# The first load of each slot in runs of 16 KB, the second in runs of 32 KB

## The chip, the cores and the metric

The kernel runs on one core of one Trainium2 chip. The metric is the device time of one execution in microseconds (us). An execution that the hardware profiler records gives a span, from the first instruction to the last, and a trace of every instruction and every DMA packet.

Five engines matter here. TensorE (PE) multiplies; VectorE (DVE) copies the products out of PSUM; ScalarE (ACT) issues the loads and moves data within SBUF; SyncE (SP) issues the stores; GpSimd (POOL) passes on that a buffer is free. Sixteen DMA engines carry the data between HBM and SBUF. ACT and SP each have a DMA queue of their own, and both queues are served by the same sixteen engines.

## The reference

For each of 128 batches one of eight weight matrices is chosen by `itok_B_0_7`, and its product is added to the input:

```python
B, C, D, T, N_SUBJECTS = (128, 128, 128, 1024, 8)
w = weights[subjects]
out = jnp.einsum('bct,bcd->bdt', x, w)
x = x + out
```

x and the output have 128 x 128 x 1024 float32 each, 67.11 MB in and 67.11 MB out. The weights are 0.52 MB.

## The kernel before

The work goes in 32 steps (`NT`) of four batches (`H * G`, two halves of two batches). One step's data is a slot: 2.10 MB of x, 16 KB in each of 128 partitions. SBUF holds 12 slots (`SLOTS`), used in turn. The product is written over the input in the same slot, and the residual is added by adding the identity matrix `eye` to the weights (line 195).

**Loads.** `load` (lines 147 to 154) issues two DMAs for a slot from ACT, one for each half h, 1 MB each. Two batches of x are one contiguous MB of HBM. `ROWS` says how the source is cut: eight rows of 4 KB make one run of 32 KB. The destination is 128 partitions with 8 KB each, so that partition p of a half has two neighbouring rows of a batch, whatever `ROWS` is. Both loads of a slot count on the same semaphore `s_in[k]`, and `landed` (line 160) waits for both.

**ACT's loop** (lines 273 to 291), for each slot in order: wait until the slot's loads have landed; wait on `s_empty` until the slot that is wanted next is free; issue the loads for the slot four steps ahead (`AHEAD`); then `trade` (lines 162 to 170), three copies within SBUF that bring the rows of one batch into one half. Four slots are loaded before the loop, and all of this is in ACT's program order: a slot that isn't free holds back the loads and also the trade behind them.

**PE** (lines 336 to 338) waits for the trade and the weights of a half and multiplies: eight matmuls a half, sixteen a slot. **DVE** (lines 330 to 335) copies the product of a half from PSUM into the slot (line 221) and prepares the next weights.

**Stores.** SP (lines 313 to 321) waits until a slot is finished and issues its store: 16 KB of SBUF per partition for one slot. The first store is written with another form (line 317), in rows of 4 KB. The last 12 slots are stored in pairs, and of these the last six slots in runs of 32 KB per partition (`WHOLE`). The very last store is issued on line 343.

**Free slots.** GpSimd waits for the store of each slot (line 311) and increments `s_empty`. So step i's loads, from step 12 on, wait for the store of step i - 12.

Of the kernel before, what the change touches and what calls it, by code (L numbers as in the profile page):

```python
# [30 lines left out]
G = 2  # L31
# [14 lines left out]

IDLE = 8

ROWS = 8

R = 2

# [12 lines left out]
def transfer(nc, engine, out, in_):  # L65

    later, nc._always_lower_symbolic_ap = nc._always_lower_symbolic_ap, False
    ins, outs = engine.lower_ap_dma(in_), engine.lower_ap_dma(out)  # L70
    nc._always_lower_symbolic_ap = later
    return engine.add_instruction(
        mybir.InstDMACopy(
            name=nc.get_next_instruction_name(),
            engine=engine.engine,
            ins=ins,
            outs=outs,
            mode="Copy",
            cce_op=ALU.bypass,
            queue=QUEUES[engine.engine],  # L80
        )
    )
# [3 lines left out]
def kernel(  # L86
# [60 lines left out]
    def load(k, slot, first):  # L147
        for h in range(H):
            transfer(
                nc,  # L150
                nc.scalar,
                x_all[:, bass.ds(slot * (H * G * T) + h * G * T, G * T)],
                x[bass.ds(first + h * G, G)].rearrange("h (b r) t -> (h b) (r t)", r=ROWS),
            ).then_inc(s_in[k], DMA)

    def move(out, in_):
# [66 lines left out]
    with tc.tile_critical():  # L223
# [44 lines left out]
        for i in range(AHEAD):  # L268
            load(i % AHEAD, i, i * (H * G))
# [3 lines left out]
        with nc.scalar.Fori(0, NT // AHEAD) as turn:  # L273
            for k in range(AHEAD):
                landed(k)
                with nc.scalar.If(turn < NT // AHEAD - 1):
                    empty = nc.scalar.wait_ge(s_empty, k + 1)
                    if k + 1 == AHEAD:
                        empty.then_inc(s_empty, -AHEAD)
                    load(  # L280
                        k,
                        (turn * AHEAD + (k + AHEAD)) % SLOTS,
                        nc.s_assert_within(
                            turn * (AHEAD * H * G) + (k + AHEAD) * H * G,
                            0,
                            B - H * G,
                            skip_runtime_bounds_check_because="the last turn loads nothing",
                        ),
                    )
                trade(k, (turn * AHEAD + k) % SLOTS)  # L290
            nc.scalar.wait_ge(s_moved, AHEAD * MOVES).then_inc(s_moved, -AHEAD * MOVES)
# [86 lines left out]
```

## Time and profile before

| What | us |
|---|---|
| three runs | 322.62, 322.94, 323.04 |
| their median | 322.94 |
| the profiled execution, its time | 323.06 |
| its span | 321.2 |
| PE matmuls busy | 250.1 (78%) |
| DVE busy | 181.4 (56%) |
| ACT busy | 183.6 (57%) |
| loads of x, median from issue to landing | 11.6 |

The span is what the trace covers; the profiled execution's own time is 1.9 us longer than it. The busy shares are means over the whole span and say nothing of which engine is waited for. The windows of the profile give the same for each stretch of time, with the busy share of the DMA engines and the rate at which they moved data as the last two columns. A packet's bytes are counted in the window in which it falls, so a rate in a short window can be off by some per cent either way.

The queue rows give, for one queue, its packets, its MB and the time that its packets took as a share of what sixteen engines have. q10 is ACT's queue, with the loads of x. q1 is SP's, with the stores, the weights and the list of subjects. Each DMA adds up to sixteen packets of 4 bytes, one from each engine, that report its completion.

### The profile page before, as it was taken

The numbers are of one execution on the slowest core, as the hardware profiler recorded it, in microseconds if no ns is written. First come the engines' busy times: TensorE is split into PE (matmuls) and PEld (weight loads), VectorE is DVE, ScalarE is ACT, GpSimd is POOL, SyncE is SP. The second block draws the span as 40 slices with busy tenths as digits, with TensorE's granted clock in tenths as the row PEclk, the third lists the DMA queues.
The fourth block names the chain that finished last, engine by engine and source line by source line (L and its number), as shares of the span: only waits on it lengthen the run. The fifth ranks groups of instructions, "written<-read, shape, count | busy, mean of one in ns | idle before, by whom it ended". The sixth has DMA issues, their size and how long they took to land. (4 is left out here: it accounts for less than half of the span.)

```text
span 321.2 us, 2576 instructions
## 1 busy us (share of the span) xinstructions
PE 250.1 (78%) x528; PEld 103.4 (32%) x528; DVE 181.4 (56%) x217; ACT 183.6 (57%) x98; POOL 2.5 (1%) x10
## 2 busy tenths in 40 slices
PE   7479998898899885949987499673997939999400
PEld 3134433333333332413433143231433414444100
DVE  4708766666677662660865627456273753877600
ACT  1577767776777726566454774547746379990000
POOL 0200000000000000000000000000000000000000
PEclk9969999999999997995999979998697998999955
DMA  8999999999999999999999999999999999999995
GB/s 314 404 457 424 420 403 436 408 433 445 426 424 426 435 414 430 437 430 441 433 402 426 416 433 441 428 418 422 426 439 441 408 453 408 426 445 418 433 428 228
DMA packets 7732, 134.76 MB, mean 420 GB/s; under 512 B 1457, under 2 KB 1458, under 8 KB 2098
## 3 DMA queue, kind: packets, MB, share of 16 engines
q1 hardware_dynamic: 4658, 67.64, 49.9%
q10 hardware_dynamic: 3072, 67.11, 49.0%
q14 instruction: 2, 0.02, 0.0%
HBM read 67.63 MB, written 67.11 MB: 419 GB/s over the span
## 5 line engine op out<-in xcount | busy, mean ns | idle before, releaser
L206 PE MATMUL ps<-x_all,w 128*128 x512 | 239.9, 627 | 48.7 <-PEq L202 48.7
L221 DVE COPY x_all<-ps 128x2048 f32 x64 | 146.6, 2291 | 116.1 <-PE ps L206 103.5
L206 PEld LDWEIGHTS ps<-x_all,w 128*128 128x128 f32 x512 | 99.3, 200 | 189.3 <-issue 189.2
L157 ACT COPY aside<-x_all 64x2048 f32 x32 | 60.7, 1897 | 95.0 <-issue 90.6
L157 ACT COPY x_all<-x_all x32 | 60.7, 1897 | 4.0
L157 ACT COPY x_all<-aside 64x2048 f32 x32 | 60.7, 1898 | 1.0
L195 DVE TENSOR_TENSOR w<-w_all,eye 128x128 f32<-128x128 f32 x132 | 31.8, 282 | 0.8 <-issue 0.8
L233 PE MATMUL ps<-x_all 128*128 128x512 f32 x16 | 10.2, 808 | 1.7 <-DVE x_all L230 1.7
L233 PEld LDWEIGHTS ps<-x_all 128*128 128x128 f32 x16 | 4.1, 262 | 6.9 <-issue 5.3
L271 ACT ACT_TABLE_LOAD x1 | 1.3, 1283 | 6.1 <-issue 6.1
L297 DVE COPY w_all<-x_all 32x256 f32<-32x256 f32 x12 | 3.9, 326 | 0.4
L242 DVE STREAM_TRANSPOSE x_all<-x_all 128x512 f32<-128x512 f32 x2 | 2.0, 1068 | 3.2 <-DMA x_all<-in_L_cond_weights_dram 3.2
L297 POOL COPY w_all<-x_all 32x256 f32<-32x256 f32 x4 | 1.7, 424 | 6.7 <-DVE x_all L294 6.6
L294 DVE STREAM_TRANSPOSE x_all<-x_all 128x1024 f32<-128x1024 f32 x1 | 1.2, 1226 | 0.0
L230 DVE MEMSET x_all<- 128x512 f32 x1 | 0.5, 485 | 1.0 <-SPq L223 1.0
L248 DVE TENSOR_SCALAR x_all<-x_all 1x128 int32<-1x128 int32 x1 | 0.2, 217 | 0.3 <-DMA x_all<-in_itok_B_dram 0.3
L258 POOL TENSOR_SCALAR_AFFINE_SELECT eye<-x_all 128x128 f32<-128x128 f32 x1 | 0.3, 292 | 1.4 <-DVE x_all L230 1.4
L252 DVE CUSTOM_DVE_ANT_0 index<-x_all 1x256 uint16<-1x256 uint16 x1 | 0.3, 280 | 0.0
L258 POOL TENSOR_SCALAR_AFFINE_SELECT eye<-eye 128x128 f32<-128x128 f32 x1 | 0.3, 292 | 0.1
L250 DVE TENSOR_SCALAR x_all<-x_all 1x128 int32<-1x128 int32 x1 | 0.2, 215 | 0.0
L271 ACT COPY mark<-eye 1x1 f32<-1x1 f32 x1 | 0.2, 190 | 0.0
L365 POOL MEMSET const-bfloat16-1.0<- 128x1 bf16 x1 | 0.1, 100 | 0.0
(5 smaller groups left out, 0.4 us busy)
## 6 DMA issues: line engine op xcount, KB each, us to landing
x_all<-in_x_dram ACTq DMA_DIRECT2D x64, 1024.0 KB, 11.6
out_dram<-x_all SPq DMA_DIRECT2D x20, 2048.0 KB, 55.0
out_dram<-x_all SPq DMA_DIRECT2D x6, 4096.0 KB, 30.9
x_all<-in_L_cond_weights_dram SPq DMA_DIRECT2D x1, 512.0 KB, 3.9
x_all<-in_itok_B_dram SPq DMA_DIRECT2D x1, 0.5 KB
```

Source lines behind the costliest of these rows:

```text
L157: nc.scalar.copy(out, in_).then_inc(s_moved, 1)
L195: copy = nc.vector.tensor_tensor(ws[q], w_all[:, bass.ds(subject[q], 1), :], eye, ALU.add)
L206: mm = nc.tensor.matmul(ps[h][:, q % G, t : t + N], ws[q][:, 0, :], x_all[:, bass.ds(at, N)], start=True, stop=True,)
L221: nc.vector.tensor_copy(mine, ps[h].rearrange("d g t -> d (g t)")).then_inc(s_added, 1)
L230: nc.vector.memset(zeros, 0.0).then_inc(s_zeros, 1)
L233: nc.tensor.matmul(ps[P_SLOTS - 1][:, G - 1, :N], zeros[:, :D], zeros, start=True, stop=True)
L242: nc.vector.transpose(w_mid.rearrange("p (e r h w j) -> p r j h e w", e=4, r=R, h=4, w=8)[:, r], w_raw.rearrange("p (j r d) -> p r j d", r ...
L252: nc.vector.tensor_tensor(index[:, :B], near, wrap, ALU.add).then_inc(s_index, 1)
L258: nc.gpsimd.affine_select(eye[:, 0], eye[:, 0] if r else zeros[:, :D], [[-1, D]], ALU.not_equal, 1.0, base=r - r * R * A, channel_multipli ...
L271: nc.scalar.copy(mark, eye[:1, 0, :1])
L294: nc.vector.transpose(w_late, w_mid).then_inc(s_sort, 1)
L297: engine.tensor_copy(w_all[32 * v : 32 * (v + 1), 2 * o : 2 * (o + 1), :], w_late[32 * o : 32 * (o + 1)].rearrange("c (e u r d) -> c u r e ...
```

## The change

`ROWS` becomes a list with a value for each half. The first load of a slot (h = 0) is cut into 64 runs of 16 KB, the second (h = 1) remains at 32 runs of 32 KB. Nothing else differs: the bytes, their places in SBUF, the order of the issues, the semaphores and their counts are the same.

```diff
-ROWS = 8
+ROWS = [4, 8]
...
                 x_all[:, bass.ds(slot * (H * G * T) + h * G * T, G * T)],
-                x[bass.ds(first + h * G, G)].rearrange("h (b r) t -> (h b) (r t)", r=ROWS),
+                x[bass.ds(first + h * G, G)].rearrange("h (b r) t -> (h b) (r t)", r=ROWS[h]),
             ).then_inc(s_in[k], DMA)
```

## The prediction

> **What bounds the kernel now.** I read the page first, its second and third parts, because they say which resource has no gaps.
>
> ```profile
> span 321.2 us, 2576 instructions
> ...
> DMA  8999999999999999999999999999999999999995
> ...
> DMA packets 7732, 134.76 MB, mean 420 GB/s; under 512 B 1457, under 2 KB 1458, under 8 KB 2098
> ...
> q1 hardware_dynamic: 4658, 67.64, 49.9%
> q10 hardware_dynamic: 3072, 67.11, 49.0%
> ...
> out_dram<-x_all SPq DMA_DIRECT2D x20, 2048.0 KB, 55.0
> ```
>
> The two queues together keep the 16 DMA engines busy for 98.9% of the span. q10 carries the loads of x: 67.11 MB, that is 64 loads of 1 MB. Its 3072 packets are 64 x 48, and 48 is 32 runs of 32 KB plus 16 completion writes (the packets under 512 B). So a packet of a load is one run of the source. q1 carries the stores and the weights; a store of 2 MB lands 55.0 us after its issue, five stores' worth of waiting. Next I read the windows, to see whether the DMA engines have slack in any stage:
>
> ```profile
> core 0: us, PE busy (x) PEld busy (x) DVE busy (x) ACT busy (x) POOL busy (x), PEclk, DMA share, GB/s
> 36.00:60.00 24.00, 21.57 (x50) 8.87 (x49) 16.72 (x21) 17.26 (x10) 0.00 (x0) 1.00 1.00 418
> 60.00:110.00 50.00, 45.94 (x105) 19.20 (x104) 34.30 (x37) 36.72 (x21) 0.00 (x0) 1.00 1.01 430
> 110.00:160.00 50.00, 38.69 (x79) 15.82 (x78) 25.81 (x31) 26.96 (x15) 0.00 (x0) 0.90 1.01 430
> 210.00:260.00 50.00, 40.32 (x82) 16.23 (x80) 27.83 (x32) 26.83 (x16) 0.00 (x0) 0.90 1.00 427
> 304.00:317.00 13.00, 0.00 (x0) 0.00 (x0) 0.00 (x0) 0.00 (x0) 0.00 (x0) 0.53 1.00 429
> 317.00:321.20 4.20, 0.00 (x0) 0.00 (x0) 0.00 (x0) 0.00 (x0) 0.00 (x0) 0.50 0.13 55
> ```
>
> The last two columns are what counts: share 1.00 or 1.01 and 418 to 430 GB/s in every stage up to 317 us, whether loads and stores are mixed or stores run alone. The compute engines have holes: PE 38.69 of 50 us in the third row, ACT 26.96. The bytes set the time: 134.76 MB at 428 GB/s are 315 us, and the rest of the span is the start and the completion of the last store.
>
> One other chain could become the bound, the one that ends in the issue of the last store. I followed it back by the timeline, the uses of line 311, and the waits of SP:
>
> ```profile
> L311 POOLq EVENT_SEMAPHORE  x1: 17/17/17, 256.1 to 256.1; - x1
> ...
> 256.47 1.16 ACTq L72 DMA_DIRECT2D x_all<-in_x_dram  x2
> 257.89 1.90 ACT L157 COPY aside<-x_all 64x2048 f32 x1 [6.32 <-issue]
> 264.12 36.39 PE L206 MATMUL ps<-x_all,w 128*128 x80 [5.04 <-PEq L202]
> 300.76 2.29 DVE L221 COPY x_all<-ps 128x2048 f32 x1 [0.79 <-DVEq L218]
> ...
> L72 SPq DMA_DIRECT2D out_dram<-x_all x25: 561/4571/12279, 36.2 to 303.7; - x25
> ...
> SPq L374 <- DMA out_dram<-x_all: 15.9, 1, 15.9
> ```
>
> At 256.1 us the store of slot 19 has landed; GpSimd passes this on (line 311), ACT issues the last two loads, then trades slot 27; PE works through five slots without a break; the last copy ends at 303.05 and SP issues the last store at 303.7. How much work the DMA engines still have then is told by the queue row of the stretch from 304 us to the end:
>
> ```profile
> q1 hardware_dynamic: 209, 5.80, 79.1%
> ```
>
> Of the 5.80 MB the last store is 4.19; 1.61 MB of the store before it had not begun, which at 427 GB/s cover 3.8 us. So the last store finds the engines busy, and this chain has slack.
>
> **The change, part by part.** Only line 153 differs. It moves no instruction, adds no wait, and leaves the bytes and their place in SBUF as they are (a slice of two batches is contiguous in HBM, however it is cut). For the 32 loads with h = 0 there are 64 runs of 16 KB in place of 32 runs of 32 KB: 32 x 32 = 1024 more packets, 64 on each of 16 engines. q10 should show 4096 packets.
>
> *The packets' price.* The trace has no load in 16 KB packets, so I bound it by the stores, which come in both sizes. These are the queue rows of three stretches with one kind of packet each: 272 to 288 us (stores in 16 KB), 292 to 312 us (stores in 32 KB), 10 to 29 us (loads in 32 KB):
>
> ```profile
> q1 hardware_dynamic: 432, 6.82, 100.2%
> ...
> q1 hardware_dynamic: 292, 8.52, 99.9%
> ...
> q10 hardware_dynamic: 383, 8.36, 102.3%
> ```
>
> 6.82 MB are 416 packets of 16 KB: 1.002 x 16 engines x 16 us / 416 = 616.6 ns each. 8.52 MB are 260 of 32 KB: 0.999 x 16 x 20 / 260 = 1229.5 ns each. Two small ones cost 2 x 616.6 - 1229.5 = 3.7 ns more than a large one. 1024 x 3.7 ns / 16 = 0.24 us. A load in 32 KB is quicker still: 1.023 x 16 x 19 / 255 = 1219.6 ns. The upper end takes the whole difference of the two queue totals as one of packet size: q1 cost 0.499 x 321.2 / 67.64 = 2.370 us per MB, q10 0.490 x 321.2 / 67.11 = 2.345; 0.0244 us x 33.55 MB (half of the loads) = 0.82 us. That includes the 4 KB packets of the weights and of the first store, so it is too high. The lower end is nothing: queues could hide the boundary. I take 0.24 us, since the same queue with the same kind of work gives it. None of it is hidden, because the engines have no gap.
>
> *The share of the two queues.* These are the rows of two stretches with both queues full: 100 to 104 us (loads in 32 KB beside stores in 16 KB) and 30 to 46 us (loads beside the first store, which goes in 4 KB rows):
>
> ```profile
> q10 hardware_dynamic: 52, 1.18, 68.8%
> q1 hardware_dynamic: 49, 0.54, 31.9%
> ...
> q10 hardware_dynamic: 271, 5.73, 84.9%
> q1 hardware_dynamic: 246, 1.01, 15.5%
> ```
>
> In the first, loads get 69% of the bytes, about 2 to 1: packet against packet. In the second, 85 to 15, near the 8 to 1 of 32 KB against 4 KB. So a shorter run takes a smaller turn. For a slot one engine's part of 128 KB will go in six turns (four of 16, two of 32 KB) in place of four, and six store packets (96 KB) pass beside it: loads get 128/224 = 57% in place of 67%, some 245 GB/s of 430 in place of 287. A slot of 2.10 MB takes 8.6 us in place of 7.3 while stores wait.
>
> The Trainium skill, page "DMA: Bandwidth & Descriptors", section "Queues, rings and completion order", also says that an engine goes round-robin between queue rows packet by packet, but its packet is typically 9 to 17 descriptors, not one run. Read so, both kinds of load would take turns of equal descriptor counts, 8 KB destination pieces against the stores' 4 KB ones, 2 to 1 before and after; the change would move no share. The trace speaks against it: 85 to 15 beside the first store, where that reading gives 67 to 33.
>
> Who waits for slower loads? These are ACT's issue of two slots' loads, and the issue row of the loads from 60 to 100 us (count, size, time to landing):
>
> ```profile
> 73.33 1.15 ACTq L72 DMA_DIRECT2D x_all<-in_x_dram  x2
> 81.01 1.15 ACTq L72 DMA_DIRECT2D x_all<-in_x_dram  x2
> ...
> x_all<-in_x_dram ACTq DMA_DIRECT2D x10, 1024.0 KB, 11.9
> ...
> ACT aside L157 <- issue: 64.2, 15, 6.3
> ```
>
> ACT asks for a slot each 7.7 us here, 273 GB/s, more than the 245 that loads will get, so they fall behind by 0.9 us a slot, 6 us over the 50 us to 110. A load is issued four slots, 31 us, before `landed` wants it, and lands 11.9 us after its issue: 19 us of cover. After 110 us (the last row is 110 to 260 us, 15 waits, 64.2 us of ACT) ACT waits for slots to be emptied; a period is there two slots' worth of bytes, 4.19 MB at 428 GB/s = 9.8 us, and a load of 8.6 us fits into it. What loads lose, stores win: they land earlier, and the engines stay full. Only without cover would ACT wait in `landed`, and even then the stores queued would keep the engines busy. At the end, store 19 lands when 20 stores and at most the 31 slots' loads issued by then have moved, as now; so the last store is issued no later than now but for the packet price. I cost the share at nothing.
>
> *Issue.* ACT's 64 issues could lengthen with more runs. SP issues its 32 KB stores, which have more pieces still, in 561 ns at least, against ACT's 501 to 512 ns: at most 0.06 us x 32 = 2 us on ACT, at least nothing. ACT's 64.2 us of waiting hide it. If the queue of loads filled up and held ACT back, as SP's issues are held (median 4571 ns), the same 19 us would cover it.
>
> **Sum.** 0.24 us on the DMA engines, nothing else. The profiled execution took 323.06 us (span 321.2, and 1.9 around it); it becomes 323.3. It lies 0.12 above the median of the three runs, 322.94, so the median becomes 323.2.
>
> **Rivals.**
> - *Dear packets (slower).* Place: every load with h = 0. Price: 0.82 us as above, 12.8 ns for each of 64 more packets on an engine; it decides from 10 ns, which makes 0.65 us. For it: no gap hides anything. Against it: 3.7 ns by the direct rows. Time 323.8.
> - *The last store comes late (slower).* If store 19 landed later than 256.1 by more than the 3.8 us of backlog less a start-up (the stores' first packets are not shown; I take 1 to 2 us), the engines would run dry before the last store. Each us beyond costs one: 1 to 2 us, 324 to 325. Against it: stores get more share, not less.
> - *The first store stops disturbing (faster).* From 36 to 60 us the engines move 418 GB/s, against 430 after: 24 x 12/430 = 0.67 us lost while the first store's 4 KB packets lie between 32 KB ones. With six turns for four it is through sooner. If all of this loss goes and packets cost nothing, 322.3; half of it with the packet price makes 322.8, no change. Against it: the small packets themselves stay.
> - *Nothing moves.* The queue cuts long runs by itself (3072 packets again), or it turns after equal counts of pieces, 8 KB of a load against 4 KB of a store, whatever the run: 322.9. Against it: packets of 32 KB as the run is now, and the 85 to 15. The second form is the Trainium skill's sentence read as above.
>
> **How the numbers follow.** A measurement of this kernel can tell about 0.2%, 0.65 us, from no change. The forecast (0.24 us, share moved, time unmoved) has 0.59; nothing moves 0.09; dear packets 0.12; a late last store 0.06; the first store 0.14. Same is 0.59 + 0.09 = 0.68, slower 0.12 + 0.06 = 0.18, faster 0.14. The range goes from the whole gain at the first store with 0.1 us for the runs' own spread, 322.2, to the dear packets with 0.3 us of a late last store, 324.1; beyond it lies most of the late store and a part of the first.
>
> **What would show it.** 4096 packets on q10 with the same MB; q10's share of the span up by about 0.1 of a point (0.24 of 321), not by 0.3; loads near 57 to 43 where both queues are full; loads landing later than 11.9 us and stores sooner than 55; DMA share still 1.00 from 60 to 317 us; SP's last issue at or before 304. Wrong would be: a DMA share under 0.98 after 300 us (late store), q10's time per MB up by over 1% (dear packets), or over 425 GB/s from 36 to 60 us with an earlier end.

## The result and the profile after

The changed kernel took 322.21 us (median of 14 runs, 321.81 to 322.96), the kernel before 322.93 us (14 runs, 322.30 to 323.17). The ratio is 0.9981, with a 95% interval of 0.9972 to 0.9989: faster by 0.19%, 0.6 us. In a second series of nine runs it was 0.9975 (0.9962 to 0.9988). The forecast was 0.24 us more. The profiled execution took 321.81 us, against 323.06.

The page of the changed kernel, its span, packets, queues and DMA issues (the last two rows end in the median time from issue to landing):

```profile
span 320.0 us, 2576 instructions
...
DMA packets 8757, 134.76 MB, mean 421 GB/s; under 512 B 1458, under 2 KB 1459, under 8 KB 2099
...
q1 hardware_dynamic: 4658, 67.64, 49.9%
q10 hardware_dynamic: 4096, 67.11, 49.3%
...
x_all<-in_x_dram ACTq DMA_DIRECT2D x64, 1024.0 KB, 15.8
out_dram<-x_all SPq DMA_DIRECT2D x20, 2048.0 KB, 55.1
```

q10 has the 4096 packets that were expected, so the change does what it says. Its packets took 0.493 x 320.0 = 157.8 us of all engines, against 0.490 x 321.2 = 157.4 before: a little more, as forecast, though the rounding of a share is worth 0.16 us in each. Loads land 4 us later. Yet the span is 1.2 us shorter. The next view is the queue rows (packets, MB, share of the 16 engines) from 60 to 100 us, first of the kernel before:

```profile
q10 hardware_dynamic: 475, 10.36, 60.4%
q1 hardware_dynamic: 472, 6.95, 40.8%
```

and of the changed one:

```profile
q10 hardware_dynamic: 552, 8.98, 52.5%
q1 hardware_dynamic: 555, 8.04, 47.3%
```

The loads' share fell from 60% to 53% of the engines' time. In both kernels the two queues have as many packets as each other, turn for turn, completions included; the loads' packets are smaller now.

Where did the time come from? The queue rows from 100 to 250 us show it. Of the kernel before:

```profile
q10 hardware_dynamic: 1485, 32.41, 50.6%
q1 hardware_dynamic: 2171, 31.64, 49.8%
```

and of the changed one:

```profile
q10 hardware_dynamic: 2071, 33.93, 52.9%
q1 hardware_dynamic: 2080, 30.41, 47.7%
```

The share times 16 engines times 150 us, divided by the MB, is what one MB costs an engine. Before: 0.506 x 2400 / 32.41 = 37.47 us for loads and 0.498 x 2400 / 31.64 = 37.78 for stores, 37.62 for both together. After: 37.42, 37.65 and 37.53. The rounding of a share is worth up to 0.04. So in these 150 us a MB became cheaper on both queues, although the loads have more packets and the stores the same ones. 0.09 us x 64.3 MB / 16 engines is 0.4 us of time.

The shares add up to slightly over 100%, so packets overlap a little, and packet time isn't quite time. The bytes say the same without it. With the bytes of each packet spread evenly over its time in the trace, the kernel before moved 64.14 MB in these 150 us and the changed one 64.32. At 428 GB/s, 0.18 MB are 0.4 us.

The engines were always busy before, but some packets took too long. The queue rows of three pairs of stretches of the kernel before show which ones; of each second stretch the loads' row alone. They are 177 to 181 and 181 to 183 us, then 137.5 to 141.3 and 141.3 to 143.3, then 255.7 to 260.4 and 260.4 to 262.4:

```profile
q1 hardware_dynamic: 115, 1.65, 99.0%
...
q10 hardware_dynamic: 19, 0.62, 80.8%
...
q1 hardware_dynamic: 101, 1.62, 100.4%
q10 hardware_dynamic: 2, 0.00, 0.0%
...
q10 hardware_dynamic: 21, 0.69, 83.9%
...
q1 hardware_dynamic: 124, 2.03, 101.6%
q10 hardware_dynamic: 11, 0.00, 0.1%
...
q10 hardware_dynamic: 19, 0.62, 72.4%
```

From 177 to 181 us there is no load at all: the loads' queue has run dry, and stores have the engines to themselves. When loads start again at 181 us, 19 of them take 0.808 x 16 x 2 us / 19 = 1361 ns each, against 1219.6 ns as usual. After the spell at 139 us it is 0.839 x 32 / 21 = 1279 ns. After the last spell it is 0.724 x 32 / 19 = 1219 ns, nothing out of the way: not every spell is followed by slow packets. By a count of the packets in its trace, the changed kernel has no stretch of even 0.8 us without a load packet between 60 and 250 us.

### The profile page after: what moved, and what is told of

It reads as the page before. It is cut to its first block, busy times and chain, and to the rows that moved or that the text cites. A ratio compares the mean times of both kernels' runs of the same rounds, so it can differ in the third digit from the quotient of the medians.

```text
span 320.0 us, 2576 instructions
## 1 busy us (share of the span) xinstructions
PE 253.6 (79%) x528; PEld 104.7 (33%) x528; DVE 181.2 (57%) x217; ACT 183.6 (57%) x98; POOL 2.5 (1%) x10
## 3 DMA queue, kind: packets, MB, share of 16 engines
q10 hardware_dynamic: 4096, 67.11, 49.3%
## 5 line engine op out<-in xcount | busy, mean ns | idle before, releaser
L206 PE MATMUL ps<-x_all,w 128*128 x512 | 244.6, 636 | 42.2 <-PEq L202 42.2
L206 PEld LDWEIGHTS ps<-x_all,w 128*128 128x128 f32 x512 | 101.0, 203 | 185.8 <-issue 185.7
L233 PE MATMUL ps<-x_all 128*128 128x512 f32 x16 | 9.0, 724 | 1.7 <-DVE x_all L230 1.7
## 6 DMA issues: line engine op xcount, KB each, us to landing
out_dram<-x_all SPq DMA_DIRECT2D x20, 2048.0 KB, 55.1
```

What stands on the lines that cost most here:

```text
L206: mm = nc.tensor.matmul(ps[h][:, q % G, t : t + N], ws[q][:, 0, :], x_all[:, bass.ds(at, N)], start=True, stop=True,)
L233: nc.tensor.matmul(ps[P_SLOTS - 1][:, G - 1, :N], zeros[:, :D], zeros, start=True, stop=True)
```

## The experiments

All times are medians of 5 to 12 runs. The kernel before ran beside them on the same chip (323.16, 323.17 and 323.12 us in the three series of four kernels). Three theories were put against each other. **A**: a load queue that starts again after a long dry spell makes packets slow, and the change removes the spells. **B**: the gain is mostly that by chance one engine ended late in the first profile. **C**: shorter packets save time by themselves, wherever both queues are full.

| Kernel | us | ratio to before (95%) | a MB from 100 to 250 us | MB moved there |
|---|---|---|---|---|
| before, again | 323.13 | 1.0000 (0.9991 to 1.0009) | 37.65 | 64.09 |
| changed, again | 322.15 | 0.9975 (0.9962 to 0.9988) | 37.51 | 64.32 |
| both loads short | 332.97 | 1.0292 (1.0267 to 1.0318) | 37.56 | 64.27 |
| second load short | 322.14 | 0.9968 (0.9955 to 0.9980) | 37.52 | 64.32 |
| long runs, issue split | 322.47 | 0.9979 (0.9970 to 0.9987) | 37.49 | 64.32 |
| long runs, issue behind the trade | 322.93 | 0.9989 (0.9979 to 0.9999) | 37.50 | 64.32 |
| changed, issue split | 322.28 | 0.9972 (0.9962 to 0.9982) | 37.53 | 64.32 |
| changed, every fourth load late | 322.18 | 0.9975 (0.9967 to 0.9984) | 37.55 | 64.32 |
| both loads short, stores in 8 KB | 323.20 | 1.0001 (0.9992 to 1.0010) | stores differ | 64.15 |
| before, stores in 8 KB | 324.33 | 1.0032 (1.0022 to 1.0042) | stores differ | 63.64 |
| changed, first store in 16 KB | 322.55 | 0.9984 (0.9976 to 0.9993) | 37.56 | 64.31 |
| before, first store in 16 KB | 323.27 | 0.9999 (0.9986 to 1.0012) | 37.62 | 64.12 |

The last two columns are worked out as above, from the two queue rows of each kernel and from the packets in its trace. The kernels with 32 KB loads issued as before stand at 37.62 to 37.65 us and 64.09 to 64.14 MB, the others with the old stores at 37.49 to 37.56 us and 64.27 to 64.32 MB. A share's rounding blurs the first of the two columns by up to 0.04; the second is the sharper one.

**The kernel before and the changed one, once more.** Both kernels as they are.

> The kernel before once more, for a second profile. Theory A (dry queue): in the first profile the loads' queue had no packet for 4.3, 4.8 and 4.7 us before 141, 181 and 221 us, and where it started again the packets of most engines took 0.1 to 0.3 us longer each, 0.46 us per engine in all from 100 to 250 us. A expects such spells and slow packets again, at least 0.25 us per engine in all. Theory B (last engine): the gain is mostly that in the first profile one engine ended 1.2 us after the others; B expects the last engine again over 1 us behind the next, whatever the slow packets do. Theory C (turns): shorter packets alone save time wherever both queues are full; C says nothing of this run. Time by all: 322.9, ratio 1.000 within 0.001.

> The changed kernel once more, for a second profile. A: again no spell without loads longer than 1 us from 60 to 250 us and under 0.05 us of slow packets per engine there. Ratio 0.997 to 0.999. Theory B (last engine): the last engine is as far behind the mean as in one of the profiles before, by chance.

The kernel before, again: queue rows from 100 to 250 us, then 157 to 161 and 161 to 163 us.

```profile
q10 hardware_dynamic: 1478, 32.18, 50.3%
q1 hardware_dynamic: 2175, 31.70, 49.9%
...
q1 hardware_dynamic: 110, 1.72, 101.3%
q10 hardware_dynamic: 2, 0.00, 0.0%
...
q10 hardware_dynamic: 20, 0.66, 83.5%
```

Spells and slow packets are there again, at other times: 0.835 x 32 / 20 = 1336 ns a packet after the spell at 159 us. So they belong to the kernel, not to one execution. The changed kernel, again, has neither:

```profile
q10 hardware_dynamic: 2076, 34.02, 53.0%
q1 hardware_dynamic: 2077, 30.34, 47.6%
```

On B: these are the windows of the last stage, from 318.5 to 319 us, of the first profile of the kernel before.

```profile
core 0: us, PE busy (x) PEld busy (x) DVE busy (x) ACT busy (x) POOL busy (x), PEclk, DMA share, GB/s
318.50:319.00 0.50, 0.00 (x0) 0.00 (x0) 0.00 (x0) 0.00 (x0) 0.00 (x0) 0.50 0.15 66
```

A share of 0.15 is one engine that began its last 32 KB packet when the others were done (a packet counts in the window in which it begins). The second profile of the same kernel has such a packet half a us earlier, from 318 to 318.5 us, and that execution took 322.51 us, against 323.06:

```profile
318.00:318.50 0.50, 0.00 (x0) 0.00 (x0) 0.00 (x0) 0.00 (x0) 0.00 (x0) 0.50 0.16 66
```

The completion writes of the last store, one from each engine, tell how late the last engine is. In the two profiles of the kernel before, their mean lies at 318.1 and 318.4 us and the last one at 319.9 and 319.3. In the two of the changed kernel the mean lies at 317.8 and 317.9, the last one at 318.6 and 318.9. So one engine ends 0.8 to 1.7 us behind the mean in all four, and of the 1.25 us between the first two profiles 0.9 is that engine. In the second profile of the kernel before it was 0.5 us behind the next engine, not over 1 as B expects. And B doesn't explain that the mean comes 0.3 to 0.5 us sooner, nor the 0.4 to 0.5 us from 100 to 250 us, which both pairs show.

**The second load short, and both.**

```diff
-ROWS = [4, 8]
+ROWS = [8, 4]
```

> The first load in runs of eight rows, the second in runs of four: the change with the halves exchanged. A and C: the same as the change, 322.2, ratio 0.997 to 0.999, no slow packets from 100 to 250 us. If it mattered that the first half gets the short runs (the first store, the start), the time would be that of before, 322.9.

It gained as the change does, so it doesn't matter which half has the short runs.

```diff
-ROWS = [4, 8]
+ROWS = [4, 4]
```

> Both loads in runs of four rows (16 KB). Loads get about 47% of the bytes where both queues are full, 10.3 us a slot, so the loads' queue is never dry between 60 and 250 us. A: the slow packets are as rare as with the change, the packet price doubles (0.13 us more): 322.2 to 322.5, ratio 0.998 to 0.999. C: the gain doubles as well: 321.5 to 321.8, ratio 0.995 to 0.997. B: as with the change or as before, by chance.

All theories missed: 2.9% slower. The views of this kernel are its queue rows from 64 to 100 us, a row of ACT's waits, windows of the last stage, GpSimd's passing on of landed stores (line 311) and SP's issues on line 72 (both from the first one's start to the last one's):

```profile
q1 hardware_dynamic: 552, 8.14, 53.2%
q10 hardware_dynamic: 556, 7.29, 47.5%
...
ACT aside L157 <- ACTq L160: 23.1, 4, 9.6
...
304.00:308.00 4.00, 1.41 (x2) 0.84 (x3) 0.00 (x0) 2.18 (x2) 0.00 (x0) 0.50 0.90 385
308.00:320.00 12.00, 8.53 (x15) 3.21 (x13) 5.39 (x6) 0.00 (x0) 0.00 (x0) 0.78 0.00 0
...
L311 POOLq EVENT_SEMAPHORE  x20: 17/17/17, 54.9 to 231.6; - x20
...
L72 SPq DMA_DIRECT2D out_dram<-x_all x25: 560/561/6153, 36.5 to 319.8; - x25
```

Loads get 47% as expected, 7.29 MB in 36 us, 10.4 us a slot. A period of 4.19 MB takes 9.8 us. So the loads fall further behind with every slot, until ACT waits in `landed` (line 160) for up to 9.6 us. The last slots are traded, multiplied and stored when nothing else is left: the DMA engines are idle for the 12 us before the last store, issued at 319.8 us. The engines run dry before the last store, as in the rival of the late last store, but not for that rival's reason: store 19 has landed by 231.6 us, 25 us sooner than before the change (256.1). It is the loads that are late; their last packet ends at 299.4 us, against 268.8. Slow packets were absent here too (37.56), which speaks for A, but a starved end costs far more than they do.

**Long runs without long spells.** ACT issues the second load of a slot behind the trade:

```diff
                 with nc.scalar.If(turn < NT // AHEAD - 1):
                     ...
-                    load(k, ...)
+                    load(k, ..., [0])
                 trade(k, (turn * AHEAD + k) % SLOTS)
+                with nc.scalar.If(turn < NT // AHEAD - 1):
+                    load(k, ..., [1])
```

> All runs of 32 KB as before, but ACT issues the first load of a slot ahead of the trade and the second behind it, some 6 us later. The turns are those of before, but the loads' queue is fed twice a slot, so its dry spells should be shorter than 4 us. A: no slow packets or few, and no packet price: 322.2 to 322.5, ratio 0.997 to 0.999. C: as before, 322.9, ratio 1.000. If landing 6 us later mattered anywhere, slower.

```profile
q10 hardware_dynamic: 1528, 33.29, 51.8%
q1 hardware_dynamic: 2109, 30.85, 48.4%
```

All packets are as long as before the change, and a MB from 100 to 250 us costs 37.49 us (the rows above), as little as with the change. The time fell by 0.21%, and 64.32 MB moved in the stretch, as many as with the change. So shorter packets are not needed for the gain: C expected nothing of this and falls here. The two together:

> The change and the split issue together. Each alone gained about 0.2 to 0.3%. A: both gain by the same thing, no dry spells, so together no more than the change: 322.0 to 322.4, ratio 0.997 to 0.998. If they gain by different things, 321.4 to 321.7, ratio 0.995.

They gain no more than the change alone, as A expects where both remove the same thing. The control has both loads behind the trade (`[0, 1]` in the second place alone):

> Runs of 32 KB as before; both loads of a slot are issued behind the trade, 6 us later, together. A control for the split issue: if the delay did it, 322.4, ratio 0.998. A: the queue is fed once a slot and runs dry as before, so slow packets and time as before: 322.9 to 323.3, ratio 0.999 to 1.001.

The time is nearly that of before, but not for A's reason. These are its queue rows from 100 to 250, from 150.6 to 154.7, from 154.7 to 156.7, and from 30 to 54 us:

```profile
q10 hardware_dynamic: 1553, 33.65, 52.4%
q1 hardware_dynamic: 2098, 30.48, 47.8%
...
q1 hardware_dynamic: 122, 1.74, 99.8%
q10 hardware_dynamic: 13, 0.00, 0.2%
...
q10 hardware_dynamic: 20, 0.66, 76.2%
...
q10 hardware_dynamic: 272, 5.77, 60.1%
q1 hardware_dynamic: 635, 3.85, 38.6%
```

From 100 to 250 us it has one long spell, and the packets after it take the usual 1219 ns; a MB costs 37.50 us. So the later issue alone evens out the spells, which was not expected, and A's forecast of them fell. It lost early what it gained: from 30 to 54 us a MB costs 0.987 x 16 x 24 / 9.62 = 39.4 us. In the kernel before it is 38.5, by these rows of the same stretch:

```profile
q10 hardware_dynamic: 361, 7.64, 76.4%
q1 hardware_dynamic: 526, 2.23, 22.6%
```

0.9 us x 9.62 MB / 16 is 0.5 us. In that stretch the stores begin; what slows the packets there was not found.

**The changed kernel with spells.** First by issuing the loads of every fourth slot behind that slot's trade.

> The changed kernel, but the loads of every fourth slot are issued behind that slot's trade, some 6 us later, so that the loads' queue runs dry once in about 40 us, for some 3 to 5 us, from about 60 us on. Runs, turns and packets are those of the change. Theory A (restart after a dry spell): slow packets come back after these spells, 0.1 to 0.25 us per engine each, three to five times: 322.5 to 323.0, ratio 0.999 to 1.001. Theory C (shorter packets as such): as the change, 322.2, ratio 0.998.

The delay left no spell after 60 us, since loads were still queued, so this test decides nothing. Then by shorter stores, which give loads the larger share again, with short loads and with long ones:

```diff
-                "d (o t) -> d o t", o=1 if i >= NT - WHOLE else n
+                "d (o t) -> d o t", o=1 if i >= NT - WHOLE else 2 * n
```

> Both loads in 16 KB runs, and the stores of single slots and of the first pairs in 8 KB runs. All packets are shorter than with the change, but loads get about 63% of the bytes where both queues are full, as before the change. Theory A (restart after a dry spell): the loads' queue has spells of 3 to 5 us without a packet again between 110 and 260 us, and slow packets after some of them, 0.2 to 0.5 us per engine in all. Theory C (shorter packets as such): no slow packets. The more numerous packets cost 0.2 to 1 us themselves, so the time, 322.6 to 323.8, tells less than the trace.

> The kernel before with the stores of single slots and of the first pairs in 8 KB runs: loads get some 74% of the bytes, so dry spells are longer and more than before the change. A: slow packets as often as before or oftener, 0.4 to 1 us per engine from 100 to 250 us; with the packets' price 323.2 to 324.2, slower than the kernel with both loads and stores short by up to 0.5.

With short loads, queue rows from 127.5 to 131.5 and from 131.6 to 133.6 us:

```profile
q1 hardware_dynamic: 209, 1.71, 101.7%
q10 hardware_dynamic: 3, 0.00, 0.0%
...
q10 hardware_dynamic: 45, 0.74, 86.0%
```

With long loads, from 166.5 to 172 and from 172 to 174 us:

```profile
q1 hardware_dynamic: 307, 2.35, 101.6%
q10 hardware_dynamic: 6, 0.00, 0.1%
...
q10 hardware_dynamic: 25, 0.82, 99.3%
```

With all packets short the spells are back, and the kernel is no faster than before, which again speaks against C, though the 8 KB stores cost something themselves. But after most of its spells the loads take the usual 0.860 x 32 / 45 = 612 ns, so A held only in part: slow packets followed two of eight. The two were its longest, 5.0 us each. With long loads the spells are longer (4.8 to 5.8 us), slow packets follow seven of eight (here 0.993 x 32 / 25 = 1271 ns), and it is the slowest kernel but one.

**The first store in the form of the others.** The branch for i = 0 with its 4 KB rows goes, in the changed kernel and in the kernel before.

> The changed kernel with the first store in the form of the others, 16 KB of SBUF per packet in place of 4 KB. From 29 to 54 us the changed kernel's packets take some 0.8 us per engine longer in all than elsewhere. If it is the 4 KB packets that do it (the rival about the first store), most of that goes: 321.4 to 321.8, ratio 0.995 to 0.997. If the load's restart at 50 us or anything else does it, no change: 322.2.

> The kernel before with the first store in the form of the others. If the 4 KB packets slow their neighbours, 0.5 us less: 322.4 to 322.6, ratio 0.998 to 0.999. The dry spells from 100 to 250 us and the slow packets after them should remain by theory A.

Neither gained; the changed kernel even lost 0.4 us by it (322.55, against 322.15 and 322.18 us of the changed kernel and its variant on the same chip). The rival about the first store's small packets falls.

**All profiles together.** Counted by the packet times in the traces of all 14 profiled executions, from 100 to 250 us, a spell without any load packet of 3.5 us or more occurred 27 times. It was followed by packets that took over 0.03 us per engine too long in all in 19 cases: 17 of 19 with 32 KB loads alone, 2 of 8 with 16 KB loads alone. No shorter spell in that stretch was. Just behind it, up to 262 us, the link is looser: two spells of 4.7 and 4.9 us were followed by none, and three of 2.0 to 2.5 us by packets that took 0.04 to 0.05 us per engine too long.

What sets the long spells apart can be seen in the same traces. In all 76 spells of 0.8 us or more from 100 to 263 us the first load packet starts 3.7 to 4.0 us after ACT began to issue the load. So a spell of about 3.7 us or more is one in which the queue was already empty when ACT issued; a shorter one begins while the next load is on its way.

The slow packets also fit the gain in size. Added up from 100 to 250 us they are 0.44 and 0.55 us per engine in the two profiles of the kernel before and nothing in those of the changed one. The bytes moved there differ by 0.18 and 0.23 MB, 0.4 and 0.5 us.

## Why the prediction was wrong

**The bound** was right: the DMA engines set the time, and their share was 1.00 or slightly more from 60 to 317 us in both kernels. What was read into it was wrong. A share of 1.00 means that packets are always in flight, not that each takes its least time. The rows of before that showed this, packet times by stage, were read only where one kind of packet ran alone.

**The packets' price**, the only term of the sum, was wrong as a price in time. In packet time it was too small. In the kernel with both loads short, 16 KB loads ran alone from 10 to 29 us:

```profile
q10 hardware_dynamic: 627, 8.18, 100.7%
```

499 packets of 16 KB at 1.007 x 304 / 499 = 613.5 ns: two take 7.4 ns more than one of 32 KB (1219.6), not 3.7. Beside stores it is 5 ns, by the usual 612 and 1219 ns above. For 1024 packets these make 0.47 and 0.32 us, not 0.24. But where both queues are full the time does not show it. From 100 to 250 us half of all loads move, so half of the 0.24 us should be missing there, 0.05 MB. Yet 64.32 MB moved with 32 KB loads alone (issue split) and 64.32 with one load short; with both short it was 64.27. So "None of it is hidden, because the engines have no gap" did not hold there. Whether it is the overlap of packets (shares above 100%) that hides the price is not shown. "Dear packets" falls with the price.

**The share**, "I cost the share at nothing", is the step that failed. In place of nothing, the runs show 0.4 to 0.5 us less from 100 to 250 us. The shift itself came, in other sizes: from 60% to 53% over 40 us, where 67% and 57% had been worked out from a stretch of 4 us. An engine's turn is also taken by the 4-byte completion of each DMA: 6 turns a slot before and 8 after, against 8 packets of 16 KB and one completion of a store, give 60% and 53%, and 47% with both loads short. The reading of the Trainium skill's sentence (page "DMA: Bandwidth & Descriptors", section "Queues, rings and completion order") by which equal counts of descriptors pass would have moved no share, and falls with these rows; its packet-by-packet turn holds, with a run or a completion as the packet. The consequence was missed: a slot of loads takes 9.3 us in place of 8.1 (2.10 MB at 8.98 and 10.36 MB in 40 us), close to the period of 9.8, so the queue hardly ever runs dry. The dry spells were visible in the trace of before, but the prediction asked only whether the engines stay full, and stores filled them.

**Who waits for slower loads**: nobody, as forecast, at 53%. ACT's cover held (it waits in `landed` for 2.6 us in all, before and after). Store 19 has landed by 252.9 us in place of 256.1, and SP's last issue came earlier, at 300.7 us:

```profile
L311 POOLq EVENT_SEMAPHORE  x20: 17/17/17, 58.3 to 252.9; - x20
...
L72 SPq DMA_DIRECT2D out_dram<-x_all x25: 560/3559/13540, 36.6 to 300.7; - x25
```

So "they land earlier" was right by the clock; counted from their issue stores land no sooner (55.1 us), since they are also issued sooner. At 47% the cover is used up, and the late last store costs 10 us. The rival had the place right, engines that run dry before the last store, but not the cause: store 19 lands early there too. What brings it about is a slot of loads longer than the period, which the prediction did not work out; its "even then the stores queued would keep the engines busy" did not hold.

**The range** held the measured time, 322.21 us, by luck. Its lower end, 322.2, was the gain of the rival about the first store, and that is not where the gain came from: from 36 to 60 us the changed kernel moved 422 GB/s, short of the 425 that this rival needed, and the two kernels without the 4 KB packets did not gain.

**What stays open.** The slow packets account for 0.4 to 0.5 us; the medians differ by 0.6 to 1.0. The rest was not placed; the engine that ends last, which differs between executions, is a candidate that was only argued. Nor was it found why packets are slow after a spell, why not after each, or whether the spell itself or something that comes with it does it. SP's issue is often under way at that time, but it isn't needed: in the kernel with long loads and 8 KB stores SP issues nothing from 219 to 235 us, and the spell from 226.2 to 231.8 us is followed by slow packets all the same.

## What to carry to other kernels

Where two queues keep the DMA engines full, read the mean time of a packet and the bytes moved by stage, not the busy share alone: a queue that runs dry and starts again can make packets dearer while no engine idles. Packet times alone can mislead too, since packets overlap. Run lengths were a knob for the shares here, since the queues took turns by packet: a step of loads should take just less than a period. Just less, because beyond it (10.4 against 9.8 us here) the end starves, and a gain of 0.2% becomes a loss of 2.9%.

## What the runs showed of the hardware

Five things were not expected. Loads of 32 KB that started again after 3.5 us or more without any took 1271 to 1361 ns, in the slow cases shown, in place of 1219. Runs of 16 KB in place of half of the 32 KB ones cost no measurable time where both queues were full (64.32 MB in 150 us either way). A load's first packet started 3.7 to 4.0 us after ACT began its issue, in all 76 restarts counted. Completion writes of 4 bytes took a full turn between the queues (60%, 53% and 47% of the engines' time for 6, 8 and 10 turns). And loads of 16 KB seem to start again more smoothly than loads of 32 KB (2 of 8 spells against 17 of 19), which one pair of kernels shows and no more, and there the spells with 16 KB loads were also shorter.
